# Cross attention on one core: batch 0's keys by fifteen block products instead of direct products, with the sums for them moved to the front

## The chip, the cores and the metric

The kernel runs on one core of a Trainium2 chip. The metric is the device time of one execution in microseconds; the time given for a kernel is the median of its runs. Engines are named as in the profile: PE is the matrix engine TensorE (PEld its weight loads), DVE is VectorE, ACT is ScalarE, POOL is GpSimd (called Pool here), SP is SyncE, which issues most DMA transfers.

## What is computed

All numbers are float32. There are 16 batches, 100 query rows of width 640, a context of 718 rows of width 384 plus 4 special rows ("tokens"), and 8 heads of width 80.

```python
query = hidden @ Wq                     # 100 x 640 per batch
keyt  = enc @ Wk                        # 718 x 384 by 384 x 640
valt  = enc @ Wv
hs    = mha(query, keyt, valt)          # 8 heads, softmax over the 718 rows
ca_q1 = einsum('btc,th->bch', ca, Wq_ca)[:, indices, :]
ca_hs1 = mha(ca_q1, hidden, hidden)     # "attention 1", over the 100 rows
ca_hs2 = mha(ca_hs1 @ Wq, ca @ Wk_ca, ca @ Wv_ca)   # "attention 2", over 4 tokens
out = (hs + ca_hs2) @ Wout + b_out + hidden
```

The change concerns `keyt` of batch 0 alone: the product of the context with `Wk`.

## The kernel before

**Tiling.** The context of a batch, transposed, is held as a 3 by 3 grid of blocks: three thirds `u` of the 718 rows (240 columns each, a few rows shared) by three parts `c` of the width 384, each block 128 x 240. `Wk` has three row parts and 640 columns; the columns go in five chunks of 128 (`n` 0 to 4). Chunks 0 to 3 are seen as two column groups `g` (chunk `n` is in group `n % 2`, at place `n // 2`). So for chunks 0 to 3 the keys are a product of a 3 x 3 grid of blocks by a 3 x 2 grid, which takes 18 block products directly. The transposed keys lie in `kT`.

**Two ways to the keys.** From batch 1 on, `Keys` (lines 453 to 480) gets chunks 0 to 3 from 15 block products instead of 18. Each product multiplies one form of the context (a block or a sum or difference of blocks) with one form of the weights (likewise). `K_PLAN` (line 113) lists them in order, each with one of five PSUM banks A to E that it accumulates into and the place in the result that gets the bank's contents right after it: the first time by a copy on ACT (line 407), later by an addition on DVE (line 405), of a 128 x 480 piece. So the next product on the same bank must wait until the bank has been read. Banks come in the order A B D A B A E B A B C A B C A. Each product is two matmuls of 128 x 128 by 128 x 240, which the profile counts as four instructions. Chunk 4 is always done directly, by `last_keys` (line 691), with weights `wk4` and nine matmuls (18 instructions).

Batch 0 does all five chunks directly: `first_keys` (line 684) runs `chunk_keys` (line 661) for chunks 0 to 3 with nine matmuls each and two copies on ACT, then `last_keys`.

**Sums.** `enc_sums` (line 481) makes the context forms that are no plain blocks, by 13 instructions on Pool of 128 x 240 each; before, it is called for batches 1 to 15 only. `weight_sums` (line 502) makes the weight forms by 12 instructions on DVE of 128 x 256 each, in the order of forms 0, 11, 12, 5, 7, 13, 1, 3, 6, 10, 2, 14; form 7 reads form 5, and 13 and 3 read form 7. Five of the twelve (5, 7, 13, 3, 14) overwrite, or depend on one that overwrites, blocks of the plain weights, which `first_keys` still reads: so the call is made twice, seven sums in front of batch 0's keys and five behind.

**The start, in program order** (all of it before the loop over the batches): loads; the values of batch 0's thirds 1 and 2 on PE (line 375); token products (`k2_ps`, `m_ps`, lines 1242 and 1265) with copies on DVE (line 1273); Pool builds a masked operand from them (`keys(load_m(0))`, line 852); PE makes `y_ps` of attention 1 from it (line 880), DVE copies a part of it out (line 890; the program calls that copy `summed`); Pool multiplies for attention 1 (`scores1`, lines 905 and 912); Pool builds the operand of batch 1 (line 852 again); PE transposes the key weights (`w_ps`, line 1288), five chunks, each copied out by ACT (line 1291), the last one into `wk4`; DVE rearranges the query weights by 15 copies (lines 1299 and 1305), then seven weight sums (line 522); batch 0's keys; five weight sums; the tokens' values (`va_ps`, line 1318); the queries (`q_ps`, line 535). Then the loop begins with the scores (`s_ps`, line 716), and DVE and ACT finish attention 1's softmax, whose result PE needs for `z_ps` (line 934).

**What sets the order.** Up to line 1349 the order on each engine is set when the program is built, by a scheduler that takes, by its own estimate of times, the earliest instruction in program order among those that are ready. `tc.issue_after(summed.ins)` puts what DVE does in that block behind the copy `summed`. From line 1349 on the order is that of the program text. Engines run their queues in order. The loads at the start are kept in program order on SP: context thirds 1 and 2 of batch 0, token data, transposed query weights, context third 0, the transposed rows `xT`, and so on; batch 1's context goes into a buffer that the tokens' value weights hold until `va_ps` is done.

Of the kernel before, what the change touches and what calls it, by code (L numbers as in the profile page):

```python
# [19 lines left out]
HC = H // P  # L20
CC = CAD // P
# [32 lines left out]
for h in range(NH):  # L54
    lo = h * D
    while lo < (h + 1) * D:
        c = lo // P
# [65 lines left out]
NF = len(V_PLAN)  # L123
# [3 lines left out]
def kernel(  # L127
# [18 lines left out]
    nc = tc.nc  # L146
# [14 lines left out]
    def pair(name):  # L161
        tile = ps2.tile([P, 2, 512], F32, tag="ps2", name=name)
        return tile
# [12 lines left out]
    def psum(name):  # L176

        turn[0] += 1
        return (psumk if turn[0] % 2 else psum1)(name)
# [28 lines left out]
    def enc_tile(name):  # L208

        return inp.tile([P, NF, KT], F32, tag="enc", name=name)  # L210

    def rest_tile(name):
        return main.tile([P, len(A_REST), KT], F32, tag="rest", name=name)
# [23 lines left out]
    def a_raw(enc, u, c):  # L237
        if (u, c) in A_REST:
            return enc[1][:, A_REST[u, c]]
        return enc[0][:, A_RAW[u, c]]  # L240

    def a_form(enc, f):
        return enc[0][:, A_AT[f]]
# [8 lines left out]
    wk_sb = const.tile([P, NF, 2, P], F32, name="wk_sb")  # L252
# [11 lines left out]
    enc = enc_tile("enc_0"), rest_tile("rest_0")  # L264
# [216 lines left out]
    def enc_sums(enc):  # L481

        at = lambda f: a_form(enc, f)
        raw = lambda u, c: a_raw(enc, u - 1, c - 1)
        for out, left, right, op in (
            (at(7), raw(2, 3), raw(3, 1), ALU.add),
            (at(11), raw(3, 2), raw(3, 3), ALU.add),
            (at(8), at(11), raw(2, 3), ALU.subtract),
            (at(10), raw(1, 3), at(11), ALU.subtract),
            (at(9), raw(2, 1), raw(2, 2), ALU.add),  # L490
            (at(2), raw(1, 1), at(9), ALU.subtract),
            (at(9), at(9), raw(3, 1), ALU.subtract),
            (at(5), raw(1, 1), raw(2, 1), ALU.subtract),
            (at(5), at(5), raw(2, 3), ALU.add),
            (at(11), raw(1, 3), raw(3, 3), ALU.subtract),
            (at(11), at(11), raw(3, 1), ALU.add),
            (at(4), at(2), at(10), ALU.add),
            (at(4), at(4), raw(1, 2), ALU.add),
        ):
            nc.gpsimd.tensor_tensor(out, left, right, op)  # L500

    def weight_sums(engine, w, late=None, there={}):


        at = lambda f: there.get(f, w[:, W_AT[f]])
        raw = lambda c, g: w[:, 2 * (c - 1) + g - 1]
        for f, left, right in (
            (0, raw(1, 2), raw(1, 1)),
            (11, raw(2, 2), raw(3, 2)),
            (12, raw(3, 2), raw(3, 1)),  # L510
            (5, raw(2, 2), raw(1, 2)),
            (7, raw(3, 2), at(5)),
            (13, raw(3, 1), at(7)),
            (1, raw(2, 1), raw(3, 1)),
            (3, raw(1, 1), at(7)),
            (6, raw(2, 1), raw(1, 1)),
            (10, raw(3, 1), raw(2, 2)),
            (2, raw(1, 1), raw(2, 2)),
            (14, raw(2, 1), raw(2, 2)),
        ):  # L520
            if late is None or late == (f in (5, 7, 13, 3, 14)):
                engine.tensor_tensor(at(f), left, right, ALU.subtract)
# [138 lines left out]
    def chunk_keys(n, banks, weights, enc):  # L661
        copies = []
        for bank, thirds in zip(banks, ((0, 1), (2,))):
            for i, u in enumerate(thirds):
                for c in range(CC):
                    nc.tensor.matmul(  # L666
                        bank[:, i * KT : (i + 1) * KT],
                        weights[c],
                        a_raw(enc, u, c),
                        start=(i == 0 and c == 0),  # L670
                        stop=(c == CC - 1),
                        skip_group_check=True,
                    )
        for bank, thirds in zip(banks, ((0, 1), (2,))):
            w = len(thirds)
            copies.append(
                nc.scalar.copy(
                    kT[:, n, thirds[0] : thirds[0] + w],
                    bank[:, : w * KT].rearrange("p (u k) -> p u k", u=w),
                )  # L680
            )
        return copies

    def first_keys(enc):
        for n in range(HC - 1):
            banks = [psum(f"kT_ps_0_{n}_{k}") for k in range(2)]
            weights = [wk_sb[:, 2 * c + n % 2, n // 2] for c in range(CC)]
            chunk_keys(n, banks, weights, enc)
        last_keys(0, enc)

    def last_keys(b, enc):
        banks = pair(f"kT_ps_{b}")
        return chunk_keys(
            HC - 1,
            [banks[:, k] for k in range(2)],
            [wk4[:, c] for c in range(CC)],
            enc,
        )
# [140 lines left out]
    def load_m(b):  # L839
        if b < 2:  # L840
            return lambda c: m_sb[c][:, b * HT : (b + 1) * HT]
        mb = small.tile([P, HC, HT], F32, tag="mb", name=f"mb_{b}", bufs=2)
        nc.sync.dma_start(
            out=mb, in_=m_d[:, :, b * HT : (b + 1) * HT].rearrange("c p n -> p c n")
        )
        return lambda c: mb[:, c]

    def keys(m):

        for c, heads in enumerate(HEADS):  # L850
            n = len(heads)
            nc.gpsimd.tensor_tensor(
                m2[:, c, :n, T:],
                m(c).unsqueeze(1).to_broadcast([P, n, HT]),
                hmask[:, c, :n].unsqueeze(2).to_broadcast([P, n, HT]),
                ALU.mult,
            )
# [404 lines left out]
    for c in range(HC):  # L1262
# [13 lines left out]
        )  # L1276
        nc.sync.dma_start(out=m_d[c], in_=m_sb[c])
    second = Second(0, xT, ca_0)
    keys(load_m(0))
    summed = second.products()  # L1280
    second.copy()
# [12 lines left out]
        )  # L1294

    with tc.issue_after(summed.ins):
        for c in range(HC):
            for r in range(2):
                nc.vector.tensor_copy(
                    wq_sb[:, c, : 4 * P].rearrange("p (n r k) -> p n r k", n=RG, r=2)[  # L1300
                        :, :, r
                    ],
                    wq_in[c].rearrange("p (r n k) -> p r n k", r=2, n=RG)[:, r, :, :64],
                )
            nc.vector.tensor_copy(
                wq_sb[:, c, 4 * P :].rearrange("p (h k) -> p h k", h=NH),
                wq_in[c].rearrange("p (h k) -> p h k", h=NH)[:, :, 64:],
            )
    with tc.issue_after(summed.ins):
        weight_sums(nc.vector, wk_sb, False)  # L1310
    first_keys(enc)
    weight_sums(nc.vector, wk_sb, True)

    va = wide("va")[:, : H // 2]
    va_ps = psum("va_ps")
# [34 lines left out]
    for b in range(B):  # L1350
        p = b // 2
        e_in, now = enc, second
        enc, second = enc_next, second_next
# [320 lines left out]
```

## Time and profile before

| | |
|---|---|
| median of 3 runs | 919.59 us (919.04 to 921.23) |
| profiled execution | 919.14 us, span 917.4 us |
| granted PE clock | 0.999 |
| PE busy | 910.1 us (99%) |
| DVE busy | 692.3 us (75%) |
| ACT busy | 434.3 us (47%) |
| Pool busy | 706.2 us (77%) |

A timeline row reads: start, time from the first start to the last end of the merged instructions, engine, source line, operation, tile written <- tiles read, shape, count, and in brackets the idle time of the engine in front of it with what ended it. In a row by source line the three numbers behind the count are the shortest, median and longest duration in ns. The ends of matmuls are modelled and overlap the next start, so a stretch on PE is measured from start to start.

### The profile page before, as it was taken

To read this page: it belongs to the slowest core of one execution; us is meant where nothing else is said; L and a number is where in the kernel's file an instruction comes from. 1 tells how busy PE (TensorE), PEld (TensorE's weight loads), DVE (VectorE), ACT (ScalarE), POOL (GpSimd) and SP (SyncE) were. 2 spreads that over 40 slices of the span, in tenths; PEclk is the share of its full clock that TensorE was granted. 3 is DMA by queue.
4 is the path that set the end of the run, shared out by engine and by line. 5 is a ranking of instruction groups with operands and counts; after the bars stand their busy time and mean duration, and the time that the engine had idled before them with its cause. 6 is when DMAs were issued, how large, how long until landed. Compare 5 with 4: busy or idle time off the path is not lost.

```text
span 917.4 us, 27706 instructions
## 1 busy us (share of the span) xinstructions
PE 910.1 (99%) x11974; PEld 765.7 (83%) x11974; DVE 692.3 (75%) x1116; ACT 434.3 (47%) x836; POOL 706.2 (77%) x659
## 2 busy tenths in 40 slices
PE   9999999999999999999999999999999999999998
PEld 6988889797797979888798787988879788797966
DVE  3459795989759897795967869679785898748883
ACT  2234533737337363652737436264741737426341
POOL 5749999687968879696896969958797687966623
PEclk9999999999999999999999999999999999999999
DMA  9822112031201302230121301203130032210211
GB/s 269 272 77 78 48 32 67 26 104 53 85 28 45 85 29 78 54 100 35 47 60 54 104 32 52 55 24 106 53 81 31 24 106 53 82 46 24 61 45 39
DMA packets 50581, 62.94 MB, mean 69 GB/s; under 512 B 13682, under 2 KB 37810, under 8 KB 50460
## 3 DMA queue, kind: packets, MB, share of 16 engines
q1 hardware_dynamic: 48812, 59.18, 21.6%
q8 instruction: 94, 1.54, 0.7%
q10 hardware_dynamic: 1024, 1.15, 0.4%
q0 software_dynamic: 624, 0.85, 0.3%
q14 instruction: 27, 0.22, 0.1%
HBM read 55.59 MB, written 5.57 MB: 67 GB/s over the span
## 4 chain that ended last, share of the span: by engine, by line
PE 99%; DMA 0%; issue 0%; DVE 0%; POOL 0%; ACTq 0%; POOLq 0%
PE s_ps L716 12%; PE a_ps L1586 12%; PE v_psA L434 11%; PE v_psB L434 9%; PE k_psA L465 8%; PE kT_ps L666 8%; PE k_psB L465 7%; PE o_ps L1164 5%; PE v_psC L434 4%; PE k_psC L465 3%; PE v_ps L375 2%; PE q_ps L593 2%; PE q_ps L535 2%; PE v_psD L434 2%; PE v_psE L434 2%; PE q_psA L593 1%
## 5 line engine op out<-in xcount | busy, mean ns | idle before, releaser
L905 POOL TENSOR_TENSOR e<-ca,g 100x800 f32<-100x800 f32 x64 | 97.9, 1541 | 100.0 <-ACT kT L407 54.6
L500 POOL TENSOR_TENSOR enc<-enc 128x240 f32<-128x240 f32 x135 | 109.0, 817 | 18.3 <-DMA enc<-in_enct 11.1
L1372 DVE TENSOR_TENSOR st<-st,over 120x1600 f32<-120x1600 f32 x48 | 113.3, 2362 | 0.0
L1586 PEld LDWEIGHTS a_ps<-vs,st 120*36 120x36 f32 (+3 forms) x3072 | 109.3, 124 | 3.5 <-issue 3.4
L1586 PE MATMUL a_ps<-vs,st 120*36 120x81 f32 (+3 forms) x3072 | 111.7, 233 | 0.0
L434 PE MATMUL v_psA<-wv_sb,enc 128*120 128x320 f32 x352 | 109.3, 433 | 0.0
L1011 POOL TENSOR_TENSOR hs<-hs,hs 100x640 f32<-100x640 f32 x48 | 94.8, 1974 | 3.8
L912 POOL TENSOR_TENSOR e<-e,e 100x800 f32<-100x800 f32 x48 | 93.6, 1950 | 3.8
L1004 POOL TENSOR_TENSOR hs<-vb,p 100x640 f32<-100x640 f32 x64 | 91.1, 1433 | 3.9 <-DMA vb<-va_d 1.0
L434 PE MATMUL v_psB<-wv_sb,enc 128*120 128x320 f32 x296 | 91.8, 433 | 0.0
L465 PE MATMUL k_psA<-enc,wk_sb 128*128 128x240 f32 x360 | 89.3, 370 | 0.0
L1380 ACT ACTIVATE st<-st 120x1600 f32<-120x1600 f32 x48 | 73.9, 1539 | 29.6 <-DVE st L1372 29.0
L434 PEld LDWEIGHTS v_psA<-wv_sb,enc 128*120 128x120 f32 x352 | 64.2, 183 | 25.0 <-DVE vs L405 0.5
L465 PEld LDWEIGHTS k_psA<-enc,wk_sb 128*128 128x128 f32 x360 | 67.2, 190 | 15.2 <-issue 0.2
L1384 DVE TENSOR_TENSOR most<-most,st 120x800 f32<-120x800 f32 x64 | 65.0, 1015 | 15.4 <-ACT st L766 14.2
L716 PE MATMUL s_ps<-qp,kT 64*56 64x100 f32 (+1 forms) x3072 | 73.1, 248 | 0.0
L465 PE MATMUL k_psB<-enc,wk_sb 128*128 128x240 f32 x300 | 73.0, 366 | 0.0
L434 PEld LDWEIGHTS v_psB<-wv_sb,enc 128*120 128x120 f32 x296 | 54.1, 183 | 21.9 <-DVE vs L405 0.4
L716 PEld LDWEIGHTS s_ps<-qp,kT 64*56 64x56 f32 (+1 forms) x3072 | 66.9, 130 | 5.4 <-issue 4.2
L1079 ACT COPY hsT<-turned_hs 32x160 f32<-32x160 f32 (+7 forms) x244 | 67.7, 278 | 3.0
L772 ACT COPY st<-s_ps 120x800 f32<-120x800 f32 x64 | 49.8, 830 | 34.3 <-PE s_ps L716 34.3
L465 PEld LDWEIGHTS k_psB<-enc,wk_sb 128*128 128x128 f32 x300 | 57.0, 190 | 7.7
(200 smaller groups left out, 1847.0 us busy)
## 6 DMA issues: line engine op xcount, KB each, us to landing
vb<-va_d SPq DMA_DIRECT2D x62, 250.0 KB
enc<-in_enct SPq DMA_DIRECT2D x30, 240.0 KB
enc<-in_enct SPq DMA_DIRECT2D x15, 360.0 KB
xT<-in_xt SPq DMA_DIRECT2D x8, 500.0 KB
rest<-in_enct SPq DMA_DIRECT2D x31, 120.0 KB
xn<-in_x SPq DMA_DIRECT2D x11, 320.0 KB
out<-xn SPq DMA_DIRECT2D x11, 320.0 KB
ca<-in_cas SPq DMA_DIRECT2D x16, 156.2 KB
```

The costliest lines, as they stand in the source:

```text
L434: nc.tensor.matmul(at[0][j][:KN, : H // 2], a_form(self.enc, f)[:, j * KN : (j + 1) * KN], wv_there.get(f, wv_sb[:, W_AT[f]]), start=first ...
L465: nc.tensor.matmul(at[:, i * KT : (i + 1) * KT], wk_sb[:, W_AT[f], i], a_form(self.enc, f), start=(first and i == 0), stop=last, skip_grou ...
L500: nc.gpsimd.tensor_tensor(out, left, right, op)
L666: nc.tensor.matmul(bank[:, i * KT : (i + 1) * KT], weights[c], a_raw(enc, u, c), start=(i == 0 and c == 0), stop=(c == CC - 1), skip_group ...
L716: nc.tensor.matmul(s_ps[at][k0:k1, cols], w, rhs, start=not begun & {(at, k) for k in range(k0, k1, 32)}, stop=last, skip_group_check=True,)
L905: first = nc.gpsimd.tensor_tensor(to, self.ca[:, t, :].unsqueeze(1).to_broadcast([S, NH, S]), g[:, :, t].unsqueeze(2).to_broadcast([S, NH, ...
L912: nc.gpsimd.tensor_tensor(e, e, to, ALU.add)
L1004: first = nc.gpsimd.tensor_tensor(to, self.vb[t][:S].rearrange("p (h d) -> p h d", h=NH), p2[:, :, t].unsqueeze(2).to_broadcast([S, NH, D] ...
L1011: nc.gpsimd.tensor_tensor(sums, sums, to, ALU.add)
L1372: return nc.vector.tensor_tensor(st[i], st[i], top.over[:KN].unsqueeze(1).to_broadcast([KN, 2, ROWS]), ALU.subtract,)
L1380: nc.scalar.activation(st[i], st[i], AF.Exp, scale=SCALE)
L1586: nc.tensor.matmul(a_v[lo:hi, h % 4], st[i // 2][: KEYS[i], i % 2, h * S + lo : h * S + hi], block(i, h // 4)[: KEYS[i], h % 4], start=(i ...
```

## The change

Batch 0's chunks 0 to 3 go through `Keys(0, enc).go(NF)`, all 15 products in a row, as no other batch's do; chunk 4 (`last_keys`) now stands in front of them. `first_keys` is gone. `enc_sums(enc)` is called for batch 0 too, and stands in front of Pool's building of the masked operand. As nothing reads the plain blocks of the key weights any more that are overwritten, `weight_sums` is one call of twelve, and it stands in front of the query weights' copies on DVE. The loop over the batches is unchanged.

```diff
@@
-    def first_keys(enc):
-        for n in range(HC - 1):
-            banks = [psum(f"kT_ps_0_{n}_{k}") for k in range(2)]
-            weights = [wk_sb[:, 2 * c + n % 2, n // 2] for c in range(CC)]
-            chunk_keys(n, banks, weights, enc)
-        last_keys(0, enc)
@@
     second = Second(0, xT, ca_0)
+    enc_sums(enc)
     keys(load_m(0))
     summed = second.products()
     second.copy()
@@
     with tc.issue_after(summed.ins):
+        weight_sums(nc.vector, wk_sb)
         for c in range(HC):
...
-    with tc.issue_after(summed.ins):
-        weight_sums(nc.vector, wk_sb, False)
-    first_keys(enc)
-    weight_sums(nc.vector, wk_sb, True)
+    last_keys(0, enc)
+    Keys(0, enc).go(NF)
```

## The prediction

> **What bounds the kernel.** I read the page first (span, busy times, chain), then the TensorE timeline of the first 110 us, then the other engines over the same stretch. The page, and one window (busy us of PE, PEld, DVE, ACT, POOL, then the clock):
>
> ```profile
> span 917.4 us, 27706 instructions
> PE 910.1 (99%) x11974; PEld 765.7 (83%) x11974; DVE 692.3 (75%) x1116; ACT 434.3 (47%) x836; POOL 706.2 (77%) x659
> PE 99%; DMA 0%; issue 0%; DVE 0%; POOL 0%; ACTq 0%; POOLq 0%
> ...
> 30.00:910.00 880.00, 879.29 (x11770) 742.62 (x11769) 680.75 (x1090) 429.12 (x826) 690.94 (x614) 1.00 0.21 62
> ```
>
> The chain that ended last is 99% TensorE (PE), and between 30 and 910 us PE is busy 879.29 of 880 us at a granted clock of 1.00. There is no slack on PE behind 30 us: each microsecond of PE work taken out there, or of waiting put in, should reach the end one for one. So I count PE time alone, and ask of the others only whether they make PE wait. The stretch that changes, from the PE timeline:
>
> ```profile
> 29.52 0.34 PE L880 MATMUL y_ps<-m,xT 128*64 128x72 f32 x4 [0.66 <-POOL m L852]
> 29.79 1.53 PE L1288 MATMUL w_ps<-ident,kT 128*128 128x128 f32 x12
> 31.15 1.38 PE L666 MATMUL kT_ps<-enc,wk_sb 128*128 128x240 f32 x6
> ...
> 45.74 1.38 PE L666 MATMUL kT_ps<-enc,wk 128*128 128x240 f32 x6
> ...
> 49.48 1.84 PE L1318 MATMUL va_ps<-wvca,tokens 128*64 128x320 f32 x12
> 51.24 8.73 PE L535 MATMUL q_ps<-xT,wq_sb 128*128 128x200 f32 x50
> ...
> 66.77 0.75 PE L934 MATMUL z_ps<-y_sb,e 100*32 100x33 f32 x64
> ...
> 81.38 0.97 PE L465 MATMUL k_psA<-enc,wk_sb 128*128 128x240 f32 x4
> 82.19 0.97 PE L465 MATMUL k_psB<-enc,wk_sb 128*128 128x240 f32 x4
> ...
> 86.24 0.97 PE L465 MATMUL k_psA<-enc,wk_sb 128*128 128x240 f32 x4
> 87.05 1.38 PE L666 MATMUL kT_ps<-enc,wk 128*128 128x240 f32 x6
> ```
>
> Batch 0's chunks 0 to 3 run from 31.15 to 45.74, chunk 4 from there to 49.48, back to back. From 81.38 the same fifteen-product plan is seen at work for batch 1: seven products (A B C A B C A) start exactly 0.81 us apart, up to 87.05.
>
> **The change, part by part.**
>
> *Products (PE).* Removed: 45.74 - 31.15 = 14.59 us. Added: 15 products x 0.81 = 12.15 us. Gain 2.44 us; that is also all the arithmetic that can be saved.
>
> *Order: chunk 4 in front.* Today the first key product needs only the weights of chunk 0, copied long before. Chunk 4 needs the last of the five copies on ScalarE:
>
> ```profile
> 28.90 0.48 ACT L1291 COPY wk_sb<-w_ps 128x384 f32<-128x384 f32 x1 [10.08 <-PE w_ps L1288]
> ...
> 30.41 1.26 ACT L1291 COPY wk_sb<-w_ps 128x384 f32<-128x384 f32 x3
> 31.55 0.50 ACT L1291 COPY wk<-w_ps 128x384 f32<-128x384 f32 x1
> ```
>
> That ends at 32.05; with 0.1 us to load weights PE starts at 32.15 instead of 31.15. Cost +1.0 us. The lower end is 0 (something else fills the hole; nothing of program order behind it is ready: the tokens' values and the queries wait for copies or loads), the upper end 1.0. I take 1.0.
>
> *Reading the banks (VectorE, ScalarE).* A plan's product on a bank waits until the result before it has been read. Six of the fifteen reads are copies on ScalarE, nine are additions on VectorE:
>
> ```profile
> L405 DVE TENSOR_TENSOR kT<-k_psA,kT x45: 612/648/659, 75.3 to 852.7; 128x480 f32<-128x480 f32 x45
> L407 ACT COPY kT<-k_psA x45: 559/559/564, 69.8 to 856.6; 128x480 f32<-128x480 f32 x45
> ```
>
> 0.66 and 0.56 us are both below 0.81, so the readers keep up. A result is readable some 1.0 us after its product starts (0.97 in the rows above). With two products between uses of a bank (1.62 us of cover plus the product itself) nothing waits. Only two places have one product between: the second and third use of A (steps 4 and 6 of the plan) and of B (steps 8 and 10). Start + 1.05 + 0.66 + 0.05 = 1.76 against 1.62: 0.13 us each, estimated from those rows; 0.25 us in all. Lower end 0, upper end below among the rivals. The eight copies that this part removes from ScalarE were on no path.
>
> *Weight sums (VectorE).* The VectorE timeline:
>
> ```profile
> 29.91 0.19 DVE L890 COPY g<-y_ps 100x32 f32<-100x32 f32 x1 [1.37 <-PE y_ps L880]
> 30.02 0.48 DVE L1299 COPY wq_sb<-wq 128x256 f32<-128x256 f32 x2
> ...
> 32.71 2.44 DVE L522 TENSOR_TENSOR wk_sb<-wk_sb 128x256 f32<-128x256 f32 x7
> ...
> 45.13 3.63 DVE L522 TENSOR_TENSOR wk_sb<-wk_sb 128x256 f32<-128x256 f32 x4 [2.81 <-PE kT_ps L666]
> 48.67 1.01 DVE L807 STREAM_TRANSPOSE turned<-e 128x800 f32<-128x800 f32 x1
> ...
> 56.34 1.01 DVE L837 STREAM_TRANSPOSE over<-spread 128x800 f32<-128x800 f32 x1 [2.53 <-DMA va_d<-va]
> 57.38 0.99 DVE L924 TENSOR_TENSOR e<-e,over 100x800 f32<-100x800 f32 x1
> ```
>
> Seven sums take 2.44 us, 0.35 each; twelve 4.2 us. They need all four chunks, copied by 31.67. The fifth of them feeds the first product: 31.7 + 5 x 0.35 = 33.5, the sixth (second product) 33.8. Chunk 4 (18 instructions, 3.7 us) covers until 32.15 + 3.7 = 35.85. So 2 us of cover; I cost the sums at nothing. The fifteen query copies (30.02 to 32.71, 2.69 us) are ready before the sums can start, so I expect most of them to fill VectorE until 31.7; the rest ends by 36.9 (30.02 + 2.69 + 4.2), before the first addition at about 39.3 and long before the queries.
>
> *Context sums (Pool).* Thirteen more instructions on Pool. Its timeline, its row for such sums by source line, and one row of VectorE:
>
> ```profile
> 13.37 0.16 POOL L365 MEMSET y_sb<- 100x8 f32 x2
> 23.15 0.29 POOL L852 TENSOR_TENSOR m<-hs_sb,hmask 128x64 f32<-128x64 f32 x1 [9.63 <-DVE hs_sb L1273]
> ...
> 30.02 5.28 POOL L852 TENSOR_TENSOR m<-m,hmask 128x64 f32<-128x64 f32 x1 [0.56 <-PE y_ps L880]
> 35.26 3.03 POOL L905 TENSOR_TENSOR e<-ca,g 100x800 f32<-100x800 f32 x2
> ...
> 45.74 1.94 POOL L912 TENSOR_TENSOR e<-e,e 100x800 f32<-100x800 f32 x1
> ```
>
> ```profile
> L500 POOL TENSOR_TENSOR enc<-enc x135: 682/698/1549, 58.8 to 818.8; 128x240 f32<-128x240 f32 x135
> ```
>
> ```profile
> 27.66 0.69 DVE L1273 COPY m<-m_ps 128x512 f32<-128x512 f32 x1 [0.63 <-PE m_ps L1265]
> ```
>
> The loads: third 0 in SyncE's timeline, what had moved by 18 us, the largest load in front, and ScalarE's exponential of attention 1:
>
> ```profile
> 8.77 1.65 SPq L271 DMA_DIRECT2D enc<-in_enct x3
> ```
>
> ```profile
> DMA packets 4311, 5.09 MB, mean 283 GB/s; under 512 B 1488, under 2 KB 3287, under 8 KB 4311
> ...
> wout_sb<-in_wqt SPq DMA_DIRECT2D x1, 1600.0 KB
> ```
>
> ```profile
> 63.85 0.88 ACT L927 ACTIVATE e<-e 100x800 f32<-100x800 f32 x1
> ```
>
> 13 x 0.70 = 9.1 us, against a hole of 9.63 us. Three need only thirds 1 and 2, which PE was already reading. The others need third 0, issued at 8.77. With everything queued ahead of it on SP and ScalarE that is 1600 KB for the transposed query weights and, by the shapes in the code, 960 + 960 + 9 x 120 + 96 KB: about 4.8 MB, an estimate; 5.09 MB had moved by 18 us, so it is there by about 18. Ten sums x 0.70 end at 25. The first work behind them, ready at 23.15, moves by 2 us, but the piece on which PE waits (the y_ps row at 29.52) depends on VectorE's copy at 27.66, which ends at 28.35, so nothing is passed on. Cost 0. The queue behind: the products of attention 1 run from 35.26 to 47.68; VectorE's run in front grows from 35.15 to 36.9, so they end near 49.5, the subtraction (57.38) has 2.53 us of idle time in front of it, and ends no later than 59.5 against an exponential that ScalarE starts at 63.85 today. Covered. No DMA moves its place in a queue; the load of batch 1's context behind the tokens' values comes as much earlier as PE does.
>
> **Where VectorE and Pool meet.** The four sums at 45.13 took 3.63 us, 0.91 each instead of 0.35, while Pool ran attention 1; and Pool's instruction at 30.02 took 5.28 us instead of 0.3, until VectorE's run of copies and sums ended. So the two hold each other up. The nine new additions read one operand from PSUM and stayed between 612 and 659 ns in the 45 of the row above, with Pool 77% busy. [...]
>
> **The sum.** -14.59 + 12.15 + 1.0 + 0.25 = -1.19 us. The profiled execution took 919.14 us (span 917.4 and 1.7 around it): 919.14 - 1.19 = 917.95, so 918.0. That execution is 0.45 us under the median of the runs, 919.59; the median after may lie as much above my figure. 0.3% is 2.76 us, about what a measurement of this kernel can tell from no change: below 916.4 it is faster, above 921.9 slower.
>
> **Rivals.**
>
> *The whole gain and more.* If another order of PE covers the wait for chunk 4's weights and the banks never stall, 919.14 - 2.44 = 916.7; if the 0.66 us of the y_ps row at 29.52 also goes, 916.0. For it: batch 1 shows seven products without a stall. Against it: no ready work for the hole.
>
> *Pool breaks into the sums.* If VectorE stands idle from 30.1 to 31.7, sums first, Pool gets in with an attention-1 product (1.5 us, 3.03 for two), and again at the two sums that depend on the one before (the fifth and sixth), as at 45.13. Then the sixth ends at 31.9 + 1.4 + 1.5 + 0.4 + 1.9 + 0.4 = 37.5 against 36.66 when PE wants it: +1.0. Six sums and fifteen copies follow (2.1 + 2.69) until 42.4; the first addition, wanted at 40.3, ends at 43.1, and bank A, wanted at 41.0, is late by 2.1. Together +3.1: 921.1. For it: the 45.13 row. Against: the copies are ready and fill the gap, and from 30.02 to 35.15 an unbroken run kept Pool out.
>
> *The context sums come late on Pool: slower.* If they don't run in the hole but behind VectorE's run, the first is done at 36.9 + 0.7 = 37.6 (+1.85 for PE). The thirteenth feeds the tenth product, which PE then wants at 45.25. At 0.70 it is done at 46.0; at Pool's mean of 0.82 over the whole run
>
> ```profile
> L500 POOL TENSOR_TENSOR enc<-enc 128x240 f32<-128x240 f32 x135 | 109.0, 817 | 18.3 <-DMA enc<-in_enct 11.1
> ```
>
> at 47.5. So +2.65 to +4.1: 920.6 to 922.1. It decides once that sum is done after 47.3. For it: Pool's other stretches are nearly full. Against: the 9.63 us hole and the early landing.
>
> **How the numbers follow.** My forecast 0.62; the whole gain 0.12 (half of it past the bound); Pool among the sums 0.13; late context sums 0.13, most of which is past the bound. Faster 0.06, slower 0.14 (with a little for a pile-up of the last two), same 0.80. The range reaches down to the bound of faster, 916.4, and up through the second rival to 921.6, which leaves about 2 in 10 out.
>
> **What will show it.** In the changed profile PE should go from transposes to chunk 4 with about 1 us idle charged to ScalarE's copy, then fifteen groups of four at 0.81; va_ps should start near 48.3 (49.48 - 1.19), z_ps near 65.6; Pool's thirteen sums should lie between 13.5 and 25.5. Wrong would be: k_ps starts further apart than 0.81 with VectorE named (second rival), k_ps waiting for Pool (third), y_ps later than 29.5, or PE idle behind 70 us, where today it has none.

## The result and the profile after

The changed kernel takes 930.61 us, the median of 5 runs (929.37 to 931.95), against 919.59 before: a ratio of 1.0117 (95% interval 1.0102 to 1.0133). It is 11 us slower. The forecast of 918.0 us and its range, 916.4 to 921.6, both missed. The profiled execution took 931.38 us with a span of 929.7, which is 12.3 us longer than the span of before; the places below are counted against that.

From the page of the changed kernel the span, and the window from 30 to 910 us (busy us of PE, PEld, DVE, ACT, POOL, then the granted clock):

```profile
span 929.7 us, 27711 instructions
...
30.00:910.00 880.00, 868.91 (x11550) 732.24 (x11551) 693.39 (x1092) 426.31 (x821) 678.37 (x612) 0.99 0.21 62
```

PE's busy time in that window is 10.4 us less than before, though the end came 12 us later: it stands still. The list of PE's waits (what waited, for what: us in total, times, longest) says where:

```profile
PE k_psA L465 <- DVE wk_sb L522: 8.4, 1, 8.4
...
```

One wait for a weight sum holds 8.4 us. PE's timeline of the changed kernel at that place, and further down in the first pass of the loop:

```profile
30.30 1.53 PE L1282 MATMUL w_ps<-ident,kT 128*128 128x128 f32 x12
32.38 0.67 PE L465 MATMUL k_psD<-enc,wk_sb 128*128 128x240 f32 x2 [0.55 <-DVE wk_sb L522]
32.89 1.38 PE L666 MATMUL kT_ps<-enc,wk 128*128 128x240 f32 x6
...
45.12 1.97 PE L465 MATMUL k_psA<-enc,wk_sb 128*128 128x240 f32 x4 [8.42 <-DVE wk_sb L522]
51.87 0.57 PE L465 MATMUL k_psE<-enc,wk_sb 128*128 128x240 f32 x2
...
60.38 1.84 PE L1311 MATMUL va_ps<-wvca,tokens 128*64 128x320 f32 x12
77.67 0.75 PE L927 MATMUL z_ps<-y_sb,e 100*32 100x33 f32 x64
...
89.55 1.05 PE L465 MATMUL k_psA<-enc,wk_sb 128*128 128x240 f32 x4 [1.15 <-DVE kT L405]
...
103.81 6.99 PE L1579 MATMUL a_ps<-vs,st 120*64 120x81 f32 x192
```

Three things are to be seen. First, chunk 4 (32.89) goes ahead of the products, but for half a product (32.38) that the scheduler put in front of it, and the product behind chunk 4 waits 8.42 us for VectorE. Second, the next four and a half products, from 45.12 to 51.87, take 6.75 us; at 0.81 each they would take 3.65. The windows of the changed kernel show why (columns as above, the clock third from the end):

```profile
36.70:45.10 8.40, 0.00 (x0) 0.00 (x0) 8.40 (x6) 0.82 (x2) 7.76 (x5) 0.76 0.64 201
45.10:51.80 6.70, 6.68 (x18) 5.73 (x19) 3.33 (x13) 1.67 (x3) 0.00 (x0) 0.54 0.61 214
51.80:60.30 8.50, 8.45 (x42) 7.38 (x40) 5.18 (x10) 1.12 (x2) 0.00 (x0) 1.00 0.00 1
```

While PE stands still the granted clock drops (0.50 from 41 to 42 us), and its mean is 0.54 over the first 6.7 us of work after the gap. And third, from z_ps to a_ps, in the first pass of the loop, PE needs 26.14 us; before it was 90.79 - 66.77 = 24.02.

What VectorE does in those 8.4 us is seen only when its run of sums is set beside Pool's work. From VectorE's timeline of the changed kernel, the run as one row and then some of its sums singly:

```profile
31.83 14.57 DVE L522 TENSOR_TENSOR wk_sb<-wk_sb 128x256 f32<-128x256 f32 x12
...
32.25 1.76 DVE L522 TENSOR_TENSOR wk_sb<-wk_sb 128x256 f32<-128x256 f32 x1
...
42.98 2.08 DVE L522 TENSOR_TENSOR wk_sb<-wk_sb 128x256 f32<-128x256 f32 x1
44.98 0.41 DVE L522 TENSOR_TENSOR wk_sb<-wk_sb 128x256 f32<-128x256 f32 x1
```

and Pool's at the same times, products and additions of attention 1 for batch 0:

```profile
30.53 1.51 POOL L845 TENSOR_TENSOR m<-m,hmask 128x64 f32<-128x64 f32 x1 [0.56 <-PE y_ps L873]
32.00 1.72 POOL L898 TENSOR_TENSOR e<-ca,g 100x800 f32<-100x800 f32 x1
...
42.85 1.93 POOL L905 TENSOR_TENSOR e<-e,e 100x800 f32<-100x800 f32 x1
```

Each of the seven sums from the second (32.25) to the eighth (42.98) starts 0.13 to 0.24 us after a Pool instruction and ends 0.28 us after that one's end (32.25 + 1.76 = 34.01, 32.00 + 1.72 = 33.72): it has waited it out and then run. The two engines take strict turns, and Pool hardly pays (1.60 to 1.72 us for a product, half of 3.03 when alone): each of the seven sums waits out one of Pool's seven attention-1 instructions. The first product needs form 7. PE is released by the eighth sum, so the scheduler put that form eighth on VectorE. It ended at 45.06, when Pool had run out of attention-1 work (42.85 + 1.93 = 44.78). The next sum (44.98) takes 0.41 us.

The span of after against before, in us (starts of the named rows; the last line is the difference of the spans):

| up to | before | after | later by | added in this stretch |
|---|---|---|---|---|
| w_ps, the 12 transposes | 29.79 | 30.30 | 0.51 | start-up and y_ps |
| va_ps, behind all keys | 49.48 | 60.38 | 10.90 | 8.42 wait + 3.10 clock - 2.44 products + 1.31 rest |
| z_ps, batch 0 | 66.77 | 77.67 | 10.90 | 0 |
| a_ps, batch 0 | 90.79 | 103.81 | 13.02 | 2.12 |
| end | 917.4 | 929.7 | 12.3 | -0.7 |

### The profile page after: what moved, and what is told of

It reads as the page before. It is cut to its first block, busy times and chain, and to the rows that moved or that the text cites. A ratio compares the mean times of both kernels' runs of the same rounds, so it can differ in the third digit from the quotient of the medians.

```text
span 929.7 us, 27711 instructions
## 1 busy us (share of the span) xinstructions
PE 912.3 (98%) x11962; PEld 765.4 (82%) x11962; DVE 709.6 (76%) x1125; ACT 434.1 (47%) x834; POOL 707.8 (76%) x672
## 3 DMA queue, kind: packets, MB, share of 16 engines
q8 instruction: 94, 1.54, 0.7%
## 4 chain that ended last, share of the span: by engine, by line
PE 93%; DVE 1%; issue 0%; DVEq 0%
PE s_ps L709 12%; PE a_ps L1579 12%; PE v_psA L434 10%; PE v_psB L434 9%; PE k_psA L465 8%; PE k_psB L465 7%; PE kT_ps L666 6%; PE o_ps L1157 5%; PE v_psC L434 3%; PE k_psC L465 3%; PE q_ps L593 2%; PE q_ps L535 2%; PE v_psD L434 2%; PE v_psE L434 2%; PE q_psA L593 1%; PE k_psD L465 1%
## 5 line engine op out<-in xcount | busy, mean ns | idle before, releaser
L500 POOL TENSOR_TENSOR enc<-enc 128x240 f32<-128x240 f32 x144 | 114.1, 802 | 34.9 <-DMA enc<-in_enct 27.6
L465 PE MATMUL k_psA<-enc,wk_sb 128*128 128x240 f32 x384 | 97.0, 376 | 9.6 <-DVE wk_sb L522 8.4
L465 PEld LDWEIGHTS k_psA<-enc,wk_sb 128*128 128x128 f32 x384 | 72.6, 193 | 26.2 <-DVE wk_sb L522 8.8
L465 PE MATMUL k_psB<-enc,wk_sb 128*128 128x240 f32 x320 | 79.1, 370 | 0.4 <-DVE sm L979 0.3
L1377 DVE TENSOR_TENSOR most<-most,st 120x800 f32<-120x800 f32 x64 | 67.9, 1061 | 14.9 <-ACT st L759 13.8
L465 PEld LDWEIGHTS k_psB<-enc,wk_sb 128*128 128x128 f32 x320 | 61.5, 193 | 9.3 <-issue 0.7
```

What stands on the lines that cost most here:

```text
L465: nc.tensor.matmul(at[:, i * KT : (i + 1) * KT], wk_sb[:, W_AT[f], i], a_form(self.enc, f), start=(first and i == 0), stop=last, skip_grou ...
L1377: most_now = nc.vector.tensor_tensor(most[:KN], most[:KN], st[i][:, u], ALU.max)
```

## The experiments

Two theories of the loss stood against each other at first. The turns: VectorE's sums and Pool's attention-1 products hold each other up, and PE waits for that. The banks: fifteen products in a row without value products between them cannot be read out in time, and would be slower than the direct way however soon the sums came. The first four kernels are the changed kernel with one edit more. The next three, from "Both together" on, add one edit after another, and the last is the kernel before with one edit. Line numbers shift by a few lines between them.

**Pool kept away from the sums.** Pool's attention-1 products of batch 0 wait for VectorE's last copy of the query weights.

```diff
-    second.scores1()
     keys(load_m(1))
...
-            nc.vector.tensor_copy(
+            arranged = nc.vector.tensor_copy(
...
+    second.scores1(arranged)
...
-                elif behind:
+                if behind and (t == 0 or b == 0):
                     wait_for(first, behind)
```

> The changed kernel, with Pool's seven products and additions of attention 1 made to wait for the last query-weight copy on VectorE, which stands behind the twelve weight sums. Nothing else differs. Theory L (each weight sum has to wait for one Pool instruction of attention 1, and TensorE waits for the eighth sum): the twelve sums take 0.35 us each from start to start (4.2 us in place of 14.6), TensorE waits under 0.5 us in front of k_psA, its clock stays at 1.00, va_ps starts near 49 us (60.4 in the changed kernel), and the time falls by 10 to 12 us to 918 to 920. Theory B (fifteen products in a row wait for their banks to be read): the sums are no matter, TensorE still loses time between the products, and the time stays above 926.

Measured: 919.8 us (918.65 to 922.4), ratio to before 0.9996 (0.9985 to 1.0007), span 916.7. Rows of VectorE, Pool and PE:

```profile
31.79 4.18 DVE L522 TENSOR_TENSOR wk_sb<-wk_sb 128x256 f32<-128x256 f32 x12
```

```profile
30.49 1.51 POOL L845 TENSOR_TENSOR m<-m,hmask 128x64 f32<-128x64 f32 x1 [0.56 <-PE y_ps L873]
37.47 3.03 POOL L898 TENSOR_TENSOR e<-ca,g 100x800 f32<-100x800 f32 x2 [5.47 <-DVE wq_sb L1299]
```

```profile
36.49 0.97 PE L465 MATMUL k_psA<-enc,wk_sb 128*128 128x240 f32 x4
...
48.65 1.83 PE L1311 MATMUL va_ps<-wvca,tokens 128*64 128x320 f32 x12
```

The twelve sums take 4.18 us instead of 14.57, PE has no wait in front of the product behind chunk 4, and the products run at 0.81 but for 0.41 us in all. The turns with Pool are the cause of the 8.4 us; the banks are not. From the twelve transposes (30.25) to va_ps it is 18.40 us against 19.69 before: -1.29, where the prediction's sum had -1.19. Yet the kernel is no faster than before: start-up is 0.46 later, and z_ps to a_ps takes 24.9 us.

**The order of the text alone.** The weight sums stand behind the fifteen copies; Pool waits for nothing new.

```diff
-        weight_sums(nc.vector, wk_sb)
         for c in range(HC):
...
+        weight_sums(nc.vector, wk_sb)
```

> The changed kernel with the weight sums behind the fifteen query-weight copies on VectorE instead of in front. Theory L with a gap (Pool gets in where VectorE leaves a gap, and from then on takes turns with it): the first three sums run at 0.35 us as before the change, Pool gets in at the first sum that waits for another (the fourth), and from there the sums take 1.7 to 2.1 us each; the sum for the first product is the sixth and is done near 38 to 39 us against 36 when TensorE wants it, and later sums make it wait again; the time is between, 921 to 926. Theory U (an unbroken run of VectorE keeps Pool out, whatever the sums): all twelve sums run at 0.35 us, TensorE waits for none, 917.5 to 919. Theory B: no change, above 926.

Measured: 920.6 us (920.09 to 933.17), ratio 1.0059 (1.0021 to 1.0098), span 918.8. VectorE and Pool:

```profile
33.28 4.12 DVE L522 TENSOR_TENSOR wk_sb<-wk_sb 128x256 f32<-128x256 f32 x12
```

```profile
30.59 6.96 POOL L845 TENSOR_TENSOR m<-m,hmask 128x64 f32<-128x64 f32 x1 [0.56 <-PE y_ps L873]
```

Nothing but the order on VectorE differs, and now Pool's small instruction is held off for 6.96 us until the sums are done. Here an unbroken run of VectorE kept Pool out. The gap that I had expected at the sums that read the one before did not open: all twelve run at one pace. So the prediction's price for Pool among the sums rested on the wrong places. The order alone is no cure, however. Of the ten executions, six took 920.1 to 920.6 us at a mean granted clock of 1.00, four 930.5 to 933.2 at 0.994, which is the clock of all five executions of the changed kernel; the profile is of the first kind, and that the four had the turns is inferred from time and clock. The ratio, formed from all ten, lies therefore above that of the medians. The product stretch is right in this kernel (va_ps at 48.98), but z_ps to a_ps is 26.1 us, as in the changed kernel.

**The clock by itself.** PE gets 15 matmuls without purpose behind chunk 4, whose results nothing reads.

```diff
     last_keys(0, enc)
+    warm = pair("warm_ps")
+    for i in range(15):
+        nc.tensor.matmul(
+            warm[:, i % 2, : H // 2],
+            ident,
+            wv_sb[:, i % 6],
+            start=True,
+            stop=True,
+        )
     Keys(0, enc).go(NF)
```

> The changed kernel with fifteen idle matmuls (128x128 by 128x320, 0.54 us each, 8.1 us in all) on TensorE behind chunk 4, in the time in which it waits for the weight sum (8.4 us); their result is not used. The wait itself stays. Theory C (the clock that the throttle grants falls because TensorE stands still, so the wait is paid a second time): the clock stays at 1.00 from 36 to 52 us, the first four and a half products start 0.81 us apart instead of 1.6 to 1.8, va_ps starts 3 us earlier, and the time falls to 927 to 928. If the slow products have another cause (banks, contention of the sums): no change, 930 to 931.

Measured: 929.47 us (928.4 to 932.57), ratio 1.0108 (1.0089 to 1.0127), span 926.9. PE, and the window of the products:

```profile
36.95 8.24 PE L1307 MATMUL warm_ps<-wv_sb,ident 128*128 128x320 f32 x30
45.56 1.08 PE L465 MATMUL k_psA<-enc,wk_sb 128*128 128x240 f32 x4 [0.37 <-DVE wk_sb L522]
```

```profile
45.50:58.00 12.50, 12.39 (x60) 11.03 (x62) 8.82 (x23) 2.77 (x6) 0.00 (x0) 1.00 0.22 69
```

The sums come as late as before, but the clock stays at 1.00 and fourteen and a half products take 12.26 us (45.56 to 57.82), 0.81 each but for 0.5 us in all. From chunk 4 (33.31) to va_ps (57.82) it is 24.51 us, against 27.49 in the changed kernel: 2.98 us, the 3.1 of the table. The spans agree (2.8 us); the timed median is above the 927 to 928 us expected, and the intervals of the timed ratios of the two kernels overlap, so that the size rests on the traces.

In the changed kernel, taken by the microsecond, the granted clock is 0.99 from 40 to 41 us, in a gap that began at 36.70, and 0.50 from 41 to 42; it is 0.50 still from 50 to 51, some six us of work behind the gap, 0.86 from 51.0 to 51.8 and 1.00 from 51.8 to 52.8.

**What opens the door to Pool.** In the changed kernel VectorE makes seven copies, and then the first sum, which waits for a copy of weights by ScalarE. Theory: only a standstill of VectorE lets Pool's pending instruction in, and turns follow as long as both have work. The rival: the sums take turns with Pool whenever Pool has attention 1 ready, so they do here too. The edit lets PE transpose chunk 4's weights first; nothing keeps Pool back.

```diff
-    for c in range(HC):
+    for c in (HC - 1, *range(HC - 1)):
         w_ps = psum(f"w_ps_{c}")
```

> The changed kernel with one line changed: chunk 4 of the key weights is transposed first. Pool's attention 1 is not made to wait. With it VectorE does nine query-weight copies before the first weight sum instead of seven, so that the first sum finds its operands ready. Theory G (Pool gets between VectorE's instructions only through a moment in which VectorE stands still, as in front of the first sum in the changed kernel, and takes turns from then on): the run of copies and sums has no hole, Pool's instruction that is pending since 30.8 us is kept out until about 37.8, the twelve sums take 4.1 us, TensorE does not wait, and the time is that of the kernel with both the wait on Pool and chunk 4 first, 918.5 to 920. Rival theory A (sums take turns with Pool whenever Pool has attention 1 ready): the sums take 14 us again and the time stays at 927 to 931.

Measured: 919.45 us (915.95 to 930.22), ratio 0.998 (0.9968 to 0.9992, formed without the one execution of 930.22), span 918.1. ScalarE of the changed kernel, for comparison, the copy that the first sum waits for:

```profile
31.32 0.48 ACT L1285 COPY wk_sb<-w_ps 128x384 f32<-128x384 f32 x1
```

VectorE, Pool and PE of the experiment:

```profile
32.37 0.29 DVE L1294 COPY wq_sb<-wq 128x256 f32<-128x256 f32 x1
32.57 4.11 DVE L522 TENSOR_TENSOR wk_sb<-wk_sb 128x256 f32<-128x256 f32 x12
```

```profile
30.75 6.95 POOL L845 TENSOR_TENSOR m<-m,hmask 128x64 f32<-128x64 f32 x1 [0.56 <-PE y_ps L873]
```

```profile
48.10 1.84 PE L1311 MATMUL va_ps<-wvca,tokens 128*64 128x320 f32 x12
```

In this profile the order of the transposes removes the whole loss at the products: va_ps starts at 48.10 instead of 60.38. VectorE makes ten copies, and the first sum follows 0.20 us after the last copy's start, as one copy follows another. In the changed kernel it followed at 0.23 (31.60 to 31.83), just behind the end of ScalarE's copy (31.32 + 0.48 = 31.80), and there Pool's instruction, pending since 30.53, ended at 32.04, with attention 1 behind it. A standstill of 0.03 us, by these rows, decided over 8 us. The other traces agree with this reading. With Pool kept away the same standstill stood in front of the first sum, and Pool's instruction got in there too (30.49 + 1.51 = 32.00); but nothing was allowed to follow it, and there were no turns. In the five profiles in which it was kept out until VectorE's run of copies and sums ended, every instruction of that run starts at least 0.08 us before the one in front of it ends; the first sum of the changed kernel starts 0.06 us before (31.83 against 31.60 + 0.29).

It need not be this standstill. One of the ten executions took 930.22 us at a clock of 0.994, the others 915.95 to 920.34 at 1.00: anything that makes VectorE pause before the eighth sum may let Pool in. A pause between two copies did so in the kernel of "The loss in the loop" below. No profile of one of the slower executions was taken, so what let Pool in there is not shown. The edits that change an order make the loss rarer (five executions of five, four of ten, one of ten), and keeping Pool away removes it: in the four kernels that do, none of 37 executions was over 922.4 us or at a clock under 0.999. That the turns go on once they have begun was seen (seven of seven) and not explained.

**Both together.** Pool kept away, and chunk 4 transposed first, to get back the wait of chunk 4 too.

```diff
-    for c in range(HC):
+    for c in (HC - 1, *range(HC - 1)):
...
-    second.scores1()
...
+    second.scores1(arranged)
```

> As with the waiting attention 1 on Pool, and chunk 4 of the key weights is transposed first instead of last, so that its copy ends some 2 us before TensorE wants it. Theory L and the prediction's terms (14.59 us out, 12.15 in, 1.0 for chunk 4's copy, 0.25 for reads): the 1.0 us of idle time in front of chunk 4 goes, and the time is 1 us under the kernel with the wait on Pool alone, 917 to 918.5, against 919.6 before the change. If the products cannot follow each other at 0.81 us, it stays at or above 919.6.

Measured: 919.41 us (917.52 to 920.63), ratio 0.999 (0.998 to 0.9999), span 917.7; expected were 917 to 918.5. PE:

```profile
31.97 1.38 PE L666 MATMUL kT_ps<-enc,wk 128*128 128x240 f32 x6
...
65.48 0.75 PE L927 MATMUL z_ps<-y_sb,e 100*32 100x33 f32 x64
...
91.60 3.61 PE L1579 MATMUL a_ps<-vs,st 120*64 120x81 f32 x96
```

Chunk 4's wait is gone, z_ps is 1.29 us earlier than before (66.77), and a_ps is 0.81 later (90.79). The whole gain is lost within the first pass of the loop, at an instruction that the change does not touch.

**The loss in the loop.** In that pass VectorE's running maximum (two instructions) meets Pool's attention 1 for batch 1. The rows of before, VectorE, Pool and PE:

```profile
69.39 2.38 DVE L1384 TENSOR_TENSOR most<-most,st 120x800 f32<-120x800 f32 x2
```

```profile
72.03 3.05 POOL L905 TENSOR_TENSOR e<-ca,g 100x800 f32<-100x800 f32 x2
```

```profile
90.79 6.98 PE L1586 MATMUL a_ps<-vs,st 120*64 120x81 f32 x192
```

and of the changed kernel, VectorE and Pool:

```profile
80.25 4.97 DVE L1377 TENSOR_TENSOR most<-most,st 120x800 f32<-120x800 f32 x2
```

```profile
81.31 3.04 POOL L898 TENSOR_TENSOR e<-ca,g 100x800 f32<-100x800 f32 x2
```

Before, Pool's products happened to start 0.26 us behind the maximum's end (69.39 + 2.38 = 71.77). In the changed kernel they fall on it, and it takes 4.97 us instead of 2.38. Its second instruction starts at 81.27, 0.04 us before the first product, and ends at 85.22, 0.87 us behind the second: it waited out both. They fall on it since Pool came earlier against PE. The products start 3.64 us behind z_ps (81.31 - 77.67), where it was 5.26 (72.03 - 66.77). The context sums of batch 1 in front of them, which wait for that batch's load, start 7.68 us behind va_ps (68.06 - 60.38), where it was 9.35 (58.83 - 49.48); why that load was there sooner is open. With the longer maximum, all of VectorE's work behind it, the additions that free the product banks among it, comes later. The edit: in the first pass, Pool's attention 1 waits for the maximum; the rest is as in the kernel just shown.

```diff
         if b == 0:
-            second.scores1()
+            second.scores1(seen)
```

> The kernel with the wait on Pool and chunk 4 first, and besides, in the loop's first pass, Pool's attention 1 of batch 1 waits for VectorE's running maximum, as it does for all later batches. It aims at the stretch from z_ps to a_ps of batch 0, 24.0 us before the change and 26.1 in that kernel (PE waits 1.1 us for k_psA on VectorE's addition, 0.3 for k_psB, and some more). If these waits come from the running maximum taking turns with Pool's attention 1 (two instructions in 4.97 us in the changed kernel, 2.38 before), they go, the stretch is 24.0 again, and the time falls by 1.5 to 2 us to 917 to 918. If they come from VectorE's own load there, the stretch stays at 26 and the time at 919.4.

Measured: 917.78 us (916.41 to 919.16), ratio 0.9977 (0.9969 to 0.9986), span 916.9. PE, VectorE and Pool:

```profile
65.67 0.75 PE L927 MATMUL z_ps<-y_sb,e 100*32 100x33 f32 x64
...
89.69 6.98 PE L1579 MATMUL a_ps<-vs,st 120*64 120x81 f32 x192
```

```profile
32.14 0.50 DVE L1293 COPY wq_sb<-wq 128x256 f32<-128x256 f32 x2
...
68.45 2.01 DVE L1377 TENSOR_TENSOR most<-most,st 120x800 f32<-120x800 f32 x2
```

```profile
30.90 1.31 POOL L845 TENSOR_TENSOR m<-m,hmask 128x64 f32<-128x64 f32 x1 [0.67 <-PE y_ps L873]
...
70.69 3.04 POOL L898 TENSOR_TENSOR e<-ca,g 100x800 f32<-100x800 f32 x2 [1.18 <-ACT kT L407]
```

The maximum takes 2.01 us, and z_ps to a_ps 89.69 - 65.67 = 24.02 us, what it was before. The loss in the loop is a hold-up by the same two engines at a second place.

At the start of this kernel the copy of 32.14 began 0.08 us after the one before it had ended (32.06), and Pool's instruction, pending since 30.90, ended at 32.21. So a pause between two copies was enough to let Pool in.

**The start-up too.** In the changed kernel and in the experiments on it PE waits 0.84 or 0.85 us for y_ps's operand, because Pool builds most of batch 1's operand in front of the last piece of batch 0's; only in the profile just shown it waited 0.99 us for a load at w_ps instead, just ahead of it. The edit, to the kernel just shown, puts it behind the copies.

```diff
-    def keys(m):
+    def keys(m, behind=None):
...
+            if behind:
+                wait_for(built, behind)
...
-    keys(load_m(1))
...
     second.scores1(arranged)
+    keys(load_m(1), arranged)
```

> The kernel before this one, and Pool builds batch 1's operand behind the query-weight copies instead of in front of the last piece of batch 0's, so that TensorE does not wait for that piece (0.85 us at y_ps with the change, 0.66 without). If that wait is real time, another 0.6 to 0.85 us: 916 to 917.5, a ratio to the kernel before the change of about 0.997. If the copies, sums or attention 1 are pushed out by it, no gain: 917 to 918.

Measured: 915.99 us (915.7 to 917.74), ratio 0.9959 (0.9947 to 0.9971), span 914.1. This is faster than both kernels, by 0.41% against before. PE:

```profile
29.19 0.34 PE L875 MATMUL y_ps<-m,xT 128*64 128x72 f32 x4
29.46 1.53 PE L1282 MATMUL w_ps<-ident,kT 128*128 128x128 f32 x12
...
47.04 1.84 PE L1313 MATMUL va_ps<-wvca,tokens 128*64 128x320 f32 x12
...
88.35 6.84 PE L1581 MATMUL a_ps<-vs,st 120*64 120x81 f32 x188
```

y_ps has no wait any more and starts 0.33 us earlier than before (29.52). From the transposes to va_ps it is 17.58 us against 19.69, which is -2.11: the 2.44 of the products less 0.33 for steps at reused banks and at the borders. The two make the 2.44 us by which a_ps is earlier than before; the span is shorter by 3.3.

**The context sums by themselves.** The kernel before, with the thirteen sums for batch 0 on Pool in front; nothing uses them.

```diff
     second = Second(0, xT, ca_0)
+    enc_sums(enc)
     keys(load_m(0))
```

> The kernel before the change with the thirteen context sums of batch 0 on Pool in front of the masked operand; their results are not used, all else is as before the change. It measures the cost of this part alone. By the prediction nothing waits for it: the sums lie between 13.5 and 27 us, y_ps moves by less than 0.3 us, and the time is within 0.3% of the kernel before. If Pool's late start of the masked operand reaches TensorE, y_ps is later by 1 us or more, and the time with it.

Measured: 921.53 us (919.82 to 923.89), ratio 1.0018 (1.0009 to 1.0027), span 920.5. PE:

```profile
30.00 0.34 PE L880 MATMUL y_ps<-m,xT 128*64 128x72 f32 x4 [0.86 <-POOL m L852]
...
67.25 0.75 PE L934 MATMUL z_ps<-y_sb,e 100*32 100x33 f32 x64
...
93.90 6.99 PE L1587 MATMUL a_ps<-vs,st 120*64 120x81 f32 x192
```

VectorE:

```profile
70.33 4.98 DVE L1385 TENSOR_TENSOR most<-most,st 120x800 f32<-120x800 f32 x2
```

At y_ps they cost 0.2 us of Pool's wait (0.86 against 0.66); the rest of the 0.48 us there (0.29) was there already when the first token products started. The larger part of the cost is again in the loop: a_ps at 93.90, so 26.65 us behind z_ps instead of 24.02, with a maximum of 4.98 us. PE had shifted by half a microsecond (z_ps 67.25 against 66.77) and Pool's products started 4.15 us behind z_ps, not 5.26; that was enough to set them on the running maximum.

## Why the prediction was wrong

**The step that failed** is "Weight sums (VectorE)": "I cost the sums at nothing". It priced a sum at 0.35 us from a run of VectorE that Pool had been kept out of, and asked only when the run would end. They cost 8.42 us of waiting and 3.10 us of clock. Two of its premises fell: the copies did not quite fill VectorE until the weights were there (seven were made, then the first sum was next in VectorE's order and waited, by some 0.03 us), and the first product's form came eighth, not fifth, because the scheduler chose another order than the program's.

**The rival that named the mechanism was mis-sized.** "Pool breaks into the sums" had the right place and the right actors, at +3.1 us and a chance of 0.13. It let Pool in once at the start and again at two sums that read the one before. (By its own figures PE's first wait was 37.5 - 36.66 = 0.84, not 1.0; that is not what failed.) Measured: one break-in at the start, then a turn at each of the next seven sums, and none at dependent sums by themselves (12 sums in 4.12 us when the run is unbroken). The evidence held against it, that an unbroken run kept Pool out, was true of the run before, which began with fifteen copies that waited for nothing; the edit lets the sums in behind the seventh, the first of them waiting for ScalarE, and that broke it. Nor had the price a term for the clock.

**The additions came out as expected, and the copies were not like them.** The prediction took from the row of before (612 to 659 ns) that the additions do not suffer from Pool. So it came out: where the nine for batch 0 ran beside Pool's attention 1, in the kernel of "What opens the door to Pool", each took 0.65 or 0.66 us, and Pool's own products and additions took 1.54 and 1.89 us meanwhile (its medians in the changed kernel are 1.54 and 1.88). That the additions owe this to having one operand in SBUF is not shown: the query-weight copies read one operand in SBUF each too, and they kept Pool out. With the sums behind the fifteen copies, Pool's instruction was pending from 30.59, and VectorE made only copies until 33.28.

**A term was missing altogether**: the loop. "PE idle behind 70 us" stood among the signs of a wrong prediction and gave no number. It was 2.12 us, since before's distance of 0.26 us between the maximum's end and Pool's products is not kept by any wait. The prediction had the load of batch 1's context come "as much earlier as PE does"; in the changed kernel the sums that wait for it started 1.67 us nearer to va_ps.

**Right:** the saving in products, the wait for chunk 4 and the banks, in sum. With Pool kept away the stretch came out at -1.29 against -1.19. In that run fourteen and a half products take 48.65 - 36.49 = 12.16 us instead of 11.75, so that the banks and the border cost 0.41 where I had 0.25; the rest, 0.74, is the wait for chunk 4, less than the 1.0 I had, since PE filled half a microsecond of it with half a product. Two terms were off by 0.16 and 0.26 in opposite senses, so the sum is nearer than its parts by luck.

**Nearly right:** the context sums. They ran from 13.70 to 26.8 us in Pool's hole and kept no product waiting, so the rival of late context sums is out. They ended later than the 25 I had, because Pool waited for third 0 until 20.27 and for its next part until 21.40, not 18. At y_ps they cost 0.2 us where I had 0.

**Open:** the 0.7 us that the changed kernel regains behind a_ps, the like 0.9 us of the fastest one, and the 0.3 to 0.7 us by which the first token products start later than before in the other kernels; no run was made for any of them. What made the slower executions of the kernels with a changed order slow was not seen, and neither was why the sums take turns with Pool while the maximum waits out two products.

## What to carry to other kernels

Where VectorE and Pool both have work at the same time, ask what happens between the instructions, not only how long one takes: here an unbroken run of VectorE kept Pool out for 5 to 7 us, and a standstill of 0.03 us was followed by turns, at Pool's pace. If a product waits for such a run, put a wait in the kernel that keeps the other engine away; where the two only happen to miss each other, another execution, or an edit that shifts them by half a microsecond, can lose more than was to be gained, as here. And look at the granted clock behind a gap on PE: here 8.4 us of waiting cost 3.1 more in clock.

## What the runs showed of the hardware that was not expected

- Strict turns: seven sums of 0.35 us took 1.75 to 2.09 us each while Pool had attention-1 work, one Pool instruction to one sum. Whether the turns began was a matter of the single execution in the kernels where nothing kept Pool away (five of five, four of ten, one of ten by time and clock). In the loop the running maximum waited out two products in a row instead (3.95 us).
- An unbroken run of copies and sums kept one 0.3 us instruction of Pool out for 6.95 us (0.3 us is what Pool's other instructions of its form take), across sums that read the one before. In one of these stretches (30.59 to 33.28) VectorE made only copies, each with one operand in SBUF.
- After 8.4 us without matmuls the granted clock was 0.54 on average over 6.7 us of dense work; with 15 matmuls without purpose in the gap it stayed at 1.00.
